# Layer 2's exponentials and logarithms from one activation table, and the layernorms' reciprocal deviation by a GpSimd power

## The chip, the cores and the metric

One core of one Trainium2 chip runs the whole program. The time is the device time of a run in microseconds (us), and a kernel's figure is the median of its runs.

## The reference, cut to what matters

Four graph layers over 4096 nodes with 256 features, each closed by a residual and a layernorm.

```
_layernorm(x) = (x - mean) / sqrt(var + 1e-5)
x = _layernorm(x + L0(x, adj))                  # attention over adj, 8 heads
x = _layernorm(x + L1(x, adj))                  # (diag + adj) @ (x @ W) + b
x = _layernorm(x + L2(x, adj))                  # two steps, below
x = _layernorm(x + L3(x, adj))                  # relu(concat(x, mean of neighbours) @ W + b)

# L2, for each of two steps:
A  = top_p(softmax(q @ k.T), 0.9)               # the largest entries of a row that sum to 0.9
Xf = R @ Xf ;  Xa = A @ Xa
Z  = Z + Xf @ U1[n].T + Xa @ U2[n].T
# after both: layernorm of X + Z with gain and bias
```

## The kernel before: the parts that matter

Layer 2 works through 32 blocks of 128 rows in each of its two steps. `scores` of block b+2, `nucleus` of block b+1 and the two products of block b are interleaved. In the profile's lines, L777 is the row sum `Zs`, L780 the logarithm that starts ScalarE's chain, L765 the chain's small functions, L866 the first use of the candidate threshold `c` on VectorE, L1058 the copy `aT` that feeds TensorE's attention products at L1061. L72 to L79 is the layernorm.

```python
def layernorm(self, pool, dst, src, gain=None, bias=None):      # L65
    ...
        nc.vector.bn_stats(stats[:, q, :], src[:, q, :])
        nc.vector.bn_aggr(mv[:, q, :], stats[:, q, :])           # L74
    std = pool.tile([P, n], F32, name="ln_std")
    nc.scalar.activation(std, mv[:, :, 1], AF.Sqrt, bias=self.eps)
    nc.vector.reciprocal(rstd, std)
    for q in range(n):
        nc.vector.tensor_scalar(dst[:, q, :], src[:, q, :], mv[:, q, 0:1], rstd[:, q:q + 1],
                                op0=ALU.subtract, op1=ALU.mult)  # L79
    ...
# layer 1, for each block
    self.adj_product(work, ps, b, lambda jc: XD[:, jc])          # TensorE, L138
    nc.gpsimd.tensor_add(xb[:, 0], xb[:, 0], row)                # L606
    nc.vector.tensor_add(xb[:, 0], xb[:, 0], ps[:, :D])          # L607
    nc.vector.tensor_add(xb[:, 0], xb[:, 0], ps[:, D:])
    self.layernorm(work, xb, xb)
    ...
# layer 2
def scores(b, above):
    product(q, e, sums=zp)                                       # logits L753, exponentials L757
    nc.vector.tensor_reduce(Z, zp, AX.X, ALU.add)                # L777, Zs
    nc.scalar.activation(t, Z, AF.Ln, scale=(1 - TOP_P) / N)     # L780
    ...                                                          # small functions, L765
    nc.scalar.activation(c1, z, AF.Exp, scale=spread[:, b:b + 1])    # L789
    ...                                                          # four passes over the row, c
def nucleus(...):
    nc.vector.scalar_tensor_tensor(c, c1, 0.3, c2, ...)          # L866
    S = evaluate("S2", c)                                        # once in step 1, twice in step 2
    ...                                                          # top 40 of a row, cut
    r = small("r")                                               # two buffers in turn
    nc.vector.tensor_reduce(r, tmp, AX.X, ALU.max)               # L928
    ...
    for j in range(M):                                           # M = 16 pieces of the mask, L947
        nc.vector.scalar_tensor_tensor(ec, ec, edge[:, j:j + 1], ec, ...)
def attention(dst, e, r):
    for g in range(NB // 4):
        ...                                                      # four transposes, L1056
        nc.scalar.copy(aT, pt)                                   # L1058
        for k in range(4):
            nc.tensor.matmul(pa[:, :D], aT[:, k * P:(k + 1) * P], X[:, jc, :], ...)   # L1061
    nc.scalar.mul(dst, pa[:, :D], r)                             # L1063, reads r
def close(step, b, two):
    terms(h[:, 0], ..., two)                                     # TensorE L1081, VectorE L1083
    if step == 1:
        self.layernorm(work, h, h, gain, lnb)
        nc.vector.tensor_add(h[:, 0], h[:, 0], xb[:, 0])
        self.layernorm(work, h, h)
        nc.scalar.dma_start(xo[...], h[:, 0])                    # L1099, issued from ScalarE's queue
    ...
```

## Time and profile before

| | us |
|---|---|
| median before, 3 runs | 5526.98 (5522.69 to 5530.19) |
| profiled span | 5533.4 |
| layer 0, to its first closing layernorm | 1737.3 |
| layer 2, step 1, first to last L866 | 1325.2 |
| layer 2, step 2, first to last L866 | 1388.0 |

Half of the kernel is layer 2, a loop over blocks. What counts there is the distance of one L866 to the next, not the busy share of an engine. A timeline line holds the start, the duration, the engine, the line, the operation, out<-in and, in brackets, the idle time ahead of it and what ended it.

### The profile page before, as it was taken

How to read it: one execution, taken by the hardware profiler on the slowest of the kernel's cores; microseconds unless marked ns; L12 is line 12 of the kernel's file. 1: busy time of each engine (PE TensorE's matmuls, PEld its weight loads, DVE VectorE, ACT ScalarE, POOL GpSimd, SP SyncE). 2: the span in 40 equal slices, each digit the busy share in tenths (PEclk: the TensorE clock that was granted, in tenths of full speed). 3: DMA queues.
4: the chain of work that ended last, by engine and by line, in shares of the span. 5: the costliest groups of instructions: out<-in, count | busy, mean ns of one | idle time of the engine just before them, and what ended most of it. 6: DMA issues, size and time to landing. Idle time of an engine off the chain costs nothing. (4 is left out here: it accounts for less than half of the span.)

```text
span 5533.4 us, 72575 instructions
## 1 busy us (share of the span) xinstructions
PE 4416.8 (80%) x25835; PEld 3505.5 (63%) x25836; DVE 3492.3 (63%) x8321; ACT 3189.8 (58%) x6086; POOL 324.7 (6%) x519
## 2 busy tenths in 40 slices
PE   6899967767774997777778887876777777777799
PEld 4699967767774873555555555634555555555677
DVE  4322258878887233866666666429888888888422
ACT  4333369879994116655556666356776767676211
POOL 3344400000000100000000000000000000000000
PEclk7899989999997998899999999988999999998999
DMA  4599953332223681111111222141111111111476
GB/s 148 187 335 343 337 194 110 131 146 89 91 94 94 223 286 43 60 64 62 62 62 63 64 70 69 55 140 38 56 56 56 56 56 56 56 56 55 148 228 204
DMA packets 333886, 655.59 MB, mean 118 GB/s; under 512 B 73537, under 2 KB 146113, under 8 KB 324289
## 3 DMA queue, kind: packets, MB, share of 16 engines
q1 hardware_dynamic: 189824, 436.29, 24.3%
q10 hardware_dynamic: 112960, 113.79, 6.3%
q0 software_dynamic: 30720, 100.69, 4.8%
q8 instruction: 208, 3.41, 0.3%
q14 instruction: 174, 1.42, 0.1%
HBM read 490.46 MB, written 160.17 MB: 118 GB/s over the span
## 5 line engine op out<-in xcount | busy, mean ns | idle before, releaser
L1061 PE MATMUL ps_a<-X,aT 128*128 128x256 f32 x4096 | 1073.9, 420 | 554.6 <-ACT aT L1058 554.5
L1061 PEld LDWEIGHTS ps_a<-X,aT 128*128 128x128 f32 x4096 | 841.4, 211 | 784.1 <-ACT aT L1058 656.9
L249 PE MATMUL acc<-gm,gt 128*128 128x198 bf16 x8192 | 747.4, 250 | 254.2 <-DVE gt L244 242.4
L242 ACT ACTIVATE sg<-lpb,lc 128x1024 bf16<-128x1024 f32 x832 | 870.9, 1134 | 119.3 <-DVE gt L244 78.9
L249 PEld LDWEIGHTS <-gt 128*128 128x128 bf16 x8192 | 693.6, 98 | 307.9 <-DVE gt L244 284.8
L1058 ACT COPY aT<-ps_tp 128x512 f32<-128x512 f32 x512 | 281.0, 581 | 640.4 <-PE ps_tp L1056 639.9
L380 PE MATMUL pz<-src,ar 128*128 128x264 f32 x4096 | 549.1, 294 | 49.2 <-ACT src L337 31.9
L244 DVE TENSOR_TENSOR gt<-sg,na 128x4096 bf16<-128x4096 bf16 x208 | 474.1, 2285 | 164.6 <-ACT sg L242 164.6
L380 PEld LDWEIGHTS pz<-src,ar 128*128 128x128 f32 x4096 | 522.7, 194 | 70.3 <-ACT src L337 42.2
L811 ACT ACTIVATE ja<-e,nc 128x2048 bf16<-128x2048 f32 x256 | 509.3, 1989 | 0.0
L138 PE MATMUL ps_r<-XD,adj_piece 128*128 128x512 f32 x2048 | 500.0, 398 | 11.2 <-DMA adj_piece<-adjs 6.6
L138 PE MATMUL ps_adj<-XD,adj_piece 128*128 128x512 f32 x2048 | 492.2, 397 | 10.2 <-DMA adj_piece<-adjs 10.2
L138 PEld LDWEIGHTS ps_r<-XD,adj_piece 128*128 128x128 f32 x2048 | 378.9, 188 | 134.5 <-DVE h L1083 28.7
L138 PEld LDWEIGHTS ps_adj<-XD,adj_piece 128*128 128x128 f32 x2048 | 383.7, 189 | 93.0 <-DVE XD L113 10.9
L841 DVE SCALAR_TENSOR_TENSOR v<-e,c 128x4096 bf16<-128x4096 f32 x96 | 429.3, 4472 | 1.1
L947 DVE SCALAR_TENSOR_TENSOR e<-e,edge 128x256 f32<-128x256 f32 x1024 | 415.0, 478 | 2.0
L753 PE MATMUL ps_logit<-kT,q 64*128 64x512 f32 x1024 | 367.7, 662 | 55.0 <-ACT e L757 53.4
L372 ACT ACTIVATE nb<-a 128x512 bf16<-128x512 f32 x256 | 158.4, 630 | 356.9 <-DMA a<-in_adjt_dram 280.9
L901 DVE MAX8 cand<-v 128x8 f32<-128x256 f32 x1024 | 355.2, 411 | 3.1
L757 ACT ACTIVATE e<-ps_logit 128x1024 f32<-128x1024 f32 x256 | 261.8, 1030 | 99.0 <-PE ps_logit L753 96.3
L1056 PE MATMUL ps_tp<-ident,e 128*128 128x128 f32 x2048 | 270.8, 274 | 40.8 <-DVE e L947 40.8
L897 DVE SCALAR_TENSOR_TENSOR v<-e,hi 128x2048 f32<-128x2048 f32 x128 | 300.8, 2350 | 2.1
(288 smaller groups left out, 4786.4 us busy)
## 6 DMA issues: line engine op xcount, KB each, us to landing
adj_piece<-adjs SPq DMA_DIRECT2D x256, 512.0 KB, 5.3
adj_piece<-adjs SPq DMA_DIRECT2D x512, 256.0 KB, 3.2
a<-in_adjt_dram SPq DMA_DIRECT2D x256, 256.0 KB, 5.8
adjs<-ar POOLq DMA_DIRECT2D x256, 256.0 KB, 5.7
na<-nad SPq DMA_DIRECT2D x64, 1024.0 KB, 6.3
nad<-nb POOLq DMA_DIRECT2D x128, 256.0 KB, 5.1
lpb<-lpd ACTq DMA_DIRECT2D x32, 512.0 KB, 5.2
gmd<-gb ACTq DMA_DIRECT2D x64, 198.0 KB, 2.2
```

The lines of the kernel that those rows point to most:

```text
L138: nc.tensor.matmul(ps, a[:, k, :], rhs(jc).rearrange("p s d -> p (s d)"), start=(jc == 0), stop=(jc == self.NB - 1))
L242: nc.scalar.activation(sg[:, k, :], lpb, AF.Sign, bias=lc[:, jc, h:h + 1])
L244: nc.vector.tensor_tensor(*flat, ALU.is_gt)
L249: nc.tensor.matmul(acc[:, q, :6 * C1], gt[:, k, q * P:(q + 1) * P], gm[:, jc, hh, :], start=(jc == 0 and q % 2 == 0), stop=(jc == NB - 1 a ...
L380: nc.tensor.matmul(pz[q][:, t, :W], ar[:, q, k, :], src[:, jc, t, s], start=(jc == 0 and s == 0), stop=(jc == NB - 1 and s == 1))
L753: nc.tensor.matmul(pl[:, s, :], q[s * A:(s + 1) * A, :], kT[s * A:(s + 1) * A, c * 512:(c + 1) * 512], start=True, stop=True)
L811: nc.scalar.activation(ja, e[:, s * HALF:(s + 1) * HALF], f, bias=nc1, accum_out=fs[:, i + s:i + s + 1])
L841: nc.vector.scalar_tensor_tensor(junk, e, c, e, op0=ALU.is_ge, op1=ALU.mult, accum_out=S)
L897: nc.vector.scalar_tensor_tensor(v, ec, hi, ec, op0=ALU.is_lt, op1=ALU.mult, accum_out=sb[:, s:s + 1])
L901: nc.vector.max(cand[:, 8 * j:8 * j + 8], v[:, k * 256:(k + 1) * 256])
L947: nc.vector.scalar_tensor_tensor(ec, ec, edge[:, j:j + 1], ec, op0=ALU.is_ge, op1=ALU.mult)
L1061: nc.tensor.matmul(pa[:, :D], aT[:, k * P:(k + 1) * P], X[:, jc, :], start=(jc == 0), stop=(jc == NB - 1))
```

## The change

ScalarE's functions come in sets, and a function outside the loaded set costs a table load (221 of them, 1.283 us each, in the profile of before). The change names the one set that serves exponential and logarithm, and takes the root, which isn't in it, away from ScalarE: GpSimd adds the epsilon and raises to the power -0.5.

```diff
-        self.eps = pool.tile([P, 1], F32, name="eps")
-        nc.vector.memset(self.eps, EPS)
+        self.power = pool.tile([P, 1], F32, name="power")
+        nc.vector.memset(self.power, -0.5)
...
-        std = pool.tile([P, n], F32, name="ln_std")
-        nc.scalar.activation(std, mv[:, :, 1], AF.Sqrt, bias=self.eps)
-        nc.vector.reciprocal(rstd, std)
+        var = pool.tile([P, n], F32, name="ln_var")
+        nc.gpsimd.tensor_scalar_add(var, mv[:, :, 1], EPS)
+        nc.gpsimd.tensor_tensor(rstd, var, self.power.to_broadcast([P, n]), ALU.pow)
...
+                nc.scalar.preload_act_table_set("natural_log_exp_and_others")
                 keys(X)
```

## The prediction

> **What bounds the kernel now.** I read the page first (busy shares), then the ScalarE groups, then the timelines of VectorE, ScalarE and TensorE over one block of each of layer 2's two steps, and last the order of instructions on each engine, before against after.
>
> ```profile
> PE 4416.8 (80%) x25835; PEld 3505.5 (63%) x25836; DVE 3492.3 (63%) x8321; ACT 3189.8 (58%) x6086; POOL 324.7 (6%) x519
> ```
>
> No engine is full, so the shares don't say what a table load is worth. The ScalarE groups give their number and price:
>
> ```profile
> L780 ACT ACT_TABLE_LOAD x64 | 82.1, 1283 | 28.2 <-DVE rest L910 27.3
> L76 ACT ACT_TABLE_LOAD x60 | 77.0, 1283 | 20.2 <-DVE ln_mv L74 19.1
> L789 ACT ACT_TABLE_LOAD x60 | 77.0, 1283 | 1.1
> ...
> L757 ACT ACT_TABLE_LOAD x20 | 25.7, 1283 | 0.4
> ...
> L765 ACT ACT_TABLE_LOAD x13 | 16.7, 1283 | 0.2
> ```
>
> With four single ones that is 221 loads of 1.283 us, 283.5 us of ScalarE. Nearly all are in layer 2 (64 blocks of 128 rows, 32 in each step). Whether they cost time depends on who waits. One block of step 1, VectorE:
>
> ```profile
> 2888.27 0.16 DVE L866 SCALAR_TENSOR_TENSOR c<-c,c 128x1 f32<-128x1 f32 x1 [0.53 <-ACT c L765]
> ...
> 2915.92 0.15 DVE L777 TENSOR_REDUCE Zs<-zp 128x1 f32<-128x4 f32 x1
> ...
> 2917.57 0.42 DVE L1070 TENSOR_TENSOR two<-XD 128x256 f32<-128x256 f32 x1
> 2921.44 0.42 DVE L1071 TENSOR_TENSOR two<-two,ps_r 128x256 f32<-128x256 f32 x1 [3.46 <-PE ps_r L138]
> ```
>
> and ScalarE after it:
>
> ```profile
> 2915.27 1.28 ACT L780 ACT_TABLE_LOAD   x1
> 2916.57 0.20 ACT L780 ACTIVATE t<-Zs 128x1 f32<-128x1 f32 x1
> ...
> 2918.63 0.39 ACT L765 ACTIVATE z<-z,qsp,t 128x1 f32<-128x1 f32 x1
> 2919.03 1.28 ACT L789 ACT_TABLE_LOAD   x1
> 2920.33 0.29 ACT L789 ACTIVATE c<-z,spread 128x1 f32<-128x1 f32 x1
> ...
> 2932.24 0.39 ACT L765 ACTIVATE c<-S,c,ri 128x1 f32<-128x1 f32 x1
> ```
>
> This is a loop over two engines. VectorE works without a gap from c (L866, 2888.27) to the row sum Zs (L777, done 2916.07): 27.8 us. Then ScalarE needs 16.6 us to make the next block's c (2932.63), and VectorE starts L866 at 2932.66. Together 44.4 us, the spacing of L866 through most of step 1. TensorE waits about 8 us in each block for ScalarE's first copy aT, which sits behind the same ScalarE chain. So the loads lie on the path.
>
> In step 2 (two evaluations per block and two layernorms) the loop is the same in kind, with four to six loads per block, and L866 comes at alternating distances of 48.6 and 43.55 us (26 blocks from 3905.70 to 5103.22, mean 46.06):
>
> ```profile
> 4322.39 0.16 DVE L866 SCALAR_TENSOR_TENSOR c<-c,c 128x1 f32<-128x1 f32 x1 [8.46 <-ACT c L765]
> ...
> 4343.86 0.14 DVE L777 TENSOR_REDUCE Zs<-zp 128x1 f32<-128x4 f32 x1
> ```
>
> **What the Trainium skill says.** (1) "ScalarE: Activation LUTs", section "What ACT_TABLE_LOAD costs": about 1283 ns for the load plus about 1380 ns of drain for every switch of set. The trace has 1283 ns exactly, but not the drain: the activation before the load at L789 ends at 2919.02, the load starts at 2919.03, and the next activation 0.02 us after it. I count 1.28 us, not 2.66. (2) Same page, "Table sets: the hidden batching unit": one set holds both exponential and logarithm, the root is in another. The trace agrees: a load stands before Ln, before Exp and before the layernorm's root, none between exponentials and the cheap functions. (3) "GPSIMD Engine Reference", section "Performance versus the Vector engine": GpSimd dispatches each instruction in software and runs a two-input add of 2048 columns in 4497 ns. Here 256 and 528 columns took 746 and 1116 ns: a line through them has 1.36 ns per column and about 0.4 us fixed, and for 128x1 only the fixed part counts. No run so far shows a power. (4) Same page, "Key points": it shares SBUF interfaces with VectorE. The trace shows signs: while GpSimd's additions ran in layer 1, VectorE's normalization (L79) took 0.61 and 1.05 us against 0.41 elsewhere.
>
> ```profile
> L345 POOL TENSOR_TENSOR v<-v,gb 128x528 f32<-128x528 f32 x32 | 35.7, 1116 | 98.8 <-ACT gb L344 98.8
> ...
> L606 POOL TENSOR_TENSOR X<-X,row 128x256 f32<-128x256 f32 x32 | 22.4, 746 | 1120.9 <-DVE row L600 1120.9
> ```
>
> **The change part by part.** In program order the changed kernel has two table loads in all, both hoisted to the start of the program; the root (144 times about 0.29 us) and VectorE's reciprocal go; two GpSimd instructions per layernorm come.
>
> *Step 1.* The steady order on ScalarE, VectorE and TensorE is that of before, instruction for instruction, less two loads per block. The second load saves its 1.28 us whole, since z, c and all that follows are one dependent chain. The first began at 2915.27, before Zs was ready (2916.07), so most of it is hidden: Ln could start at about 2916.11 instead of 2916.57, which is 0.46. Together 1.74 us per block, 44.4 to 42.65. Would another loop stop it? TensorE's: aT to the last logits' exponential is 27.25 us (2888.00 to 2915.25), Zs and its handoffs 0.25, ScalarE from Ln to aT and TensorE 14.5 without the load: 42.0, just under. 28 blocks at 1.74: -49 us.
>
> *Step 2.* Here the order does change, from a pattern of two blocks to one of one block, and the row sum L777 moves behind the first layernorm. I add up the new loop with the durations of before. VectorE from c to the second L897: 17.9 us; to L915: 5.0; from there, interleaved top-8 searches and layernorm, to the end of L777: 4.0; sum 26.9, plus a stall s1 where L79 waits for GpSimd. ScalarE from Zs: Ln and two small activations 0.9, a DMA issue, two more; then a DMA issue of xo that waits for the second layernorm's output, so that Exp starts 3.4 + s2 after Ln; from Exp to c 12.24 as before plus a 0.40 copy (L1073) that now stands there. Sum 43.0 + s1 + s2. With P the time from the statistics' end to the reciprocal deviation back on VectorE, 0.33 and 0.54 us of other VectorE work cover it: s1 = P - 0.33, s2 = P - 0.54. So the loop is 42.15 + 2P. P, an estimate: handoffs 0.2 and 0.15 (row to GpSimd in layer 1 took 0.23, GpSimd to GpSimd 0.07), the addition 0.25, the power 0.4 fixed plus 0.2 for its arithmetic: 1.2 us. The loop becomes 44.55 against 46.06: 1.5 us per block, 29 blocks, -44 us. Of about 6 us of loads per block only a quarter would come back: part was already hidden, part is given to GpSimd's round trip and to the later row sum.
>
> *Starts of the steps.* Before the first c of each step four or five loads stand in a bare ScalarE chain (2152 to 2185 and 3682 to 3715): -5 and -6.
>
> *Elsewhere.* Layer 1: in GpSimd's queue 29 of the 32 additions of L606 (0.70 us apart from 1834.9) stand before the first layernorm's power, so VectorE would wait at L79 of block 0 until about 1856.9 instead of 1841.5. The matmuls of block 3 need the PSUM buffer of block 1, which VectorE then empties at 1858 instead of 1853.8: +4.3 us, on a stretch where TensorE is the bound and can't regain it. The last layernorms of layer 1 and layer 3: +0.6 each. The layernorms between layers 0 and 1 lose 16 reciprocals of 0.15 on a nearly full VectorE: -2.
>
> Sum: -49 - 44 - 11 + 3.5 = -100.5. 5527 - 101 = 5426 us.
>
> **The rivals.** *All 284 us (5 per cent) come back.* For it: TensorE waits for ScalarE's aT 554.5 us in all. Against: the loads before Ln overlap VectorE's work, and VectorE's 27.8 us of the loop don't shrink. At most two loads per block on the path would give about 5380. *GpSimd's power is slow* (a scalar routine, P of 2 us or more): step 2's loop is then 46.2, nothing is gained there, and the time is about 5468; at P of 3 step 2 loses 2 us per block and the kernel ends near 5520. The fixed 0.4 us of an ordinary GpSimd instruction speaks for, the never-seen power neither way. *VectorE becomes the bound and hides all*: its work in step 2 is about 39.5 us per block with bubbles, in step 1 about 30, so it still idles some microseconds; this only matters if the loop falls below that.
>
> **Range and chances.** Step 1 is nearly certain (same order, measured durations), give or take 8 us. Step 2 carries the doubt: 0.1 us of P is worth 6 us of the total. P of 0.9 gives about 5408, 1.6 about 5450. Range 5400 to 5465. The 2 per cent line is at 5416, 10 us below my number: faster 0.38, same 0.60, slower 0.02.
>
> **What would show it.** Two loads in all; L866 spaced at 42.6 in step 1, with L780 starting within 0.1 us of Zs; L866 evenly spaced at 44 to 45 in step 2; VectorE idle about 0.9 us before L79, released by GpSimd; a VectorE wait of about 15 us at the first L79 of layer 1 and about 4 us of TensorE. It is wrong if step 1 moves by other than 1.7 us per block, or the power takes over 1 us.

## More of the kernel before

Every comparison with the kernel before uses runs made beside it on the same chip. Stage lengths come from the one profiled execution of each kernel, whose span lies within 7 us of the kernel's median.

## The result, and the profile after

| | median, us | range | runs |
|---|---|---|---|
| before | 5528.18 | 5522.69 to 5530.19 | 4 |
| after | 5449.53 | 5449.14 to 5451.39 | 4 |

The ratio is 0.986, 95% interval 0.9843 to 0.9877: within 2%. A ratio here is the mean time of one kernel's runs over that of the other's of the same rounds, so it isn't quite the ratio of the medians.

All 221 table loads but two are gone, and ScalarE's busy time falls by 319 us. The kernel got 79 us shorter. This table says where. It is worked out from the timelines of the two profiles: each stage ends where the next begins.

| stage | before | after | difference | predicted |
|---|---|---|---|---|
| layer 0, to its first closing layernorm | 1737.3 | 1722.8 | -14.5 | 0 |
| layer 0's closing layernorms | 32.0 | 45.0 | +13.0 | -2 |
| to layer 1's row (L600) | 65.0 | 64.2 | -0.8 | 0 |
| layer 1, to its last L607 | 230.3 | 238.8 | +8.5 | +4.3 |
| start of step 1, to its first L866 | 120.3 | 120.8 | +0.5 | -4.4 |
| step 1, first to last L866 | 1325.2 | 1284.6 | -40.6 | -49 |
| start of step 2, to its first L866 | 205.1 | 200.2 | -4.9 | -6 |
| step 2, first to last L866 | 1388.0 | 1335.2 | -52.8 | -44 |
| end of step 2 and layer 3 | 430.2 | 435.8 | +5.6 | +0.6 |
| span | 5533.4 | 5447.4 | -86.0 | -100.5 |

The first row isn't the change's work: its code is the same in both kernels, and in the fourteen profiles it took 1722.8 to 1740.5 us. The other stages sum to -71.5 us, beside 79 us between the medians, so some 7 us are assigned to no stage. The rest of this section goes through the other rows.

**GpSimd's cost.** The page of after and its groups by form (count | busy time, mean ns of one):

```profile
PE 4418.2 (81%) x25835; PEld 3512.0 (64%) x25836; DVE 3488.5 (64%) x8177; ACT 2870.9 (53%) x5723; POOL 444.1 (8%) x807
```

```profile
L77 POOL TENSOR_TENSOR ln_rstd<-ln_var,power 128x1 f32<-128x1 f32 x128 | 72.4, 566 | 10.6
...
L77 POOL TENSOR_TENSOR ln_rstd<-ln_var,power 128x2 f32<-128x2 f32 x16 | 11.9, 741 | 1.3
L76 POOL TENSOR_SCALAR ln_var<-ln_mv 128x2 f32<-128x2 f32 x16 | 6.7, 419 | 1045.0 <-DMA X<-in_x_dram 1019.2 <-DVE ln_mv L74 25.9
```

The power takes 0.57 us for one column, as estimated. The form with two columns takes 0.74 and its addition 0.42, and that is the form of layer 0's closing layernorms. One of them, before and then after:

```profile
1755.11 0.70 DVE L79 TENSOR_SCALAR X<-X,ln_mv,ln_rstd 128x256 f32<-128x256 f32 x2
```

```profile
1755.29 0.73 DVE L79 TENSOR_SCALAR X<-X,ln_mv,ln_rstd 128x256 f32<-128x256 f32 x2 [0.91 <-POOL ln_rstd L77]
```

VectorE now stands still for 0.9 us ahead of a normalization that had no wait before.

**Layer 1.** Its first layernorm and what follows it, after (GpSimd's additions, VectorE, TensorE):

```profile
1832.62 20.18 POOL L606 TENSOR_TENSOR X<-X,row 128x256 f32<-128x256 f32 x29 [65.62 <-DVE row L600]
```

```profile
1854.24 1.48 DVE L79 TENSOR_SCALAR X<-X,ln_mv,ln_rstd 128x256 f32<-128x256 f32 x1 [15.62 <-POOL ln_rstd L77]
```

```profile
1856.62 23.59 PE L138 MATMUL ps_adj<-XD,adj_piece 128*128 128x512 f32 x95 [5.14 <-issue]
```

GpSimd works through 29 additions before it comes to the first power. VectorE waits 15.6 us for it and so empties no PSUM buffer, and TensorE stops for 5.1 us. (The profile names no releaser for this stop; it is gone when the additions leave GpSimd, run adds_on_vector below.)

**Step 1.** Four L866 in a row, after:

```profile
2871.42 0.16 DVE L866 SCALAR_TENSOR_TENSOR c<-c,c 128x1 f32<-128x1 f32 x1 [0.53 <-ACT c L765]
...
2914.07 0.16 DVE L866 SCALAR_TENSOR_TENSOR c<-c,c 128x1 f32<-128x1 f32 x1 [0.53 <-ACT c L765]
...
2957.32 0.16 DVE L866 SCALAR_TENSOR_TENSOR c<-c,c 128x1 f32<-128x1 f32 x1 [0.53 <-ACT c L765]
...
3001.13 0.16 DVE L866 SCALAR_TENSOR_TENSOR c<-c,c 128x1 f32<-128x1 f32 x1 [0.53 <-ACT c L765]
```

The distances are 42.65, 43.25 and 43.81 us, and this period of three repeats through the whole step. The first is the predicted 42.65. ScalarE's part lost exactly what was predicted in all three: from the start of Zs to that of the logarithm it went from 0.65 to 0.19 us, from there to the exponential from 3.76 to 2.48. What varies is the time from L866 to Zs: 27.65, 28.26 and 28.82 us. It comes from TensorE. The first 16 attention products of the three blocks that follow:

```profile
2913.80 6.06 PE L1061 MATMUL ps_a<-X,aT 128*128 128x256 f32 x16 [6.78 <-ACT aT L1058]
...
2957.05 6.61 PE L1061 MATMUL ps_a<-X,aT 128*128 128x256 f32 x16 [6.49 <-ACT aT L1058]
...
3000.86 5.20 PE L1061 MATMUL ps_a<-X,aT 128*128 128x256 f32 x16 [5.39 <-ACT aT L1058]
```

They took 6.06, 6.61 and 5.20 us, and their blocks are the ones of 43.25, 43.81 and again 42.65; later groups of 16 take 3.72. VectorE shows how this reaches the loop, in the first and the second of these blocks:

```profile
2935.06 0.20 DVE L928 TENSOR_REDUCE r<-tmp 128x1 f32<-128x40 f32 x1 [0.16 <-ACT two L1063]
...
2978.87 0.20 DVE L928 TENSOR_REDUCE r<-tmp 128x1 f32<-128x40 f32 x1 [0.72 <-ACT two L1063]
```

L928 writes r, of which there are two buffers, and by the profile waits for ScalarE's L1063, which reads an older r once the attention products are done. After it VectorE waits 0.25 us more at L1083 for TensorE. In the blocks of 42.65 us both waits are absent. The granted clock says why the products are slow. Three stretches around the first of them (from:to, length, then the busy time of PE, weight loads, DVE, ACT, POOL; the third number from the right is PEclk):

```profile
2907.00:2911.70 4.70, 0.02 (x2) 0.00 (x0) 0.00 (x0) 4.70 (x10) 0.00 (x0) 1.00 0.00 0
2911.80:2918.40 6.60, 4.60 (x11) 3.72 (x12) 4.72 (x3) 3.18 (x12) 0.00 (x0) 0.50 0.11 42
2918.60:2922.00 3.40, 3.11 (x19) 2.58 (x18) 3.19 (x7) 1.07 (x2) 0.00 (x0) 1.00 0.00 0
```

TensorE idles from 2907.0 on. 4.7 us later the clock is halved, and it stays so for 6.8 us, well into the products that end the wait. Read in steps of 0.4 us, the halved stretches of three blocks in a row last 6.8, 10.2 and 3.4 us. The Trainium skill's page "TensorE: Matmul & The Clock Gate" (Part 1, "What's actually happening") says that the clock is halved after an idle window, and that the window is 4096 cycles at 1.2 GHz, 3413 ns, and runs free. The trace agrees: the stretches are 2, 3 and 1 times 3.41 us, and in its clock records all halved stretches of both steps begin on one grid of 3.413 us.

**Step 2.** The two layernorms of one block, after: VectorE's waits, GpSimd's pair, and ScalarE's queue:

```profile
4593.95 0.41 DVE L79 TENSOR_SCALAR h<-h,ln_mv,ln_rstd 128x256 f32<-128x256 f32 x1 [0.69 <-POOL ln_rstd L77]
...
4597.96 0.41 DVE L79 TENSOR_SCALAR h<-h,ln_mv,ln_rstd 128x256 f32<-128x256 f32 x1 [0.45 <-POOL ln_rstd L77]
```

```profile
4598.40 0.36 ACTq L1099 DMA_DIRECT2D xo<-h  x1
4598.81 0.39 ACT L765 ACTIVATE z<-z,cs,t 128x1 f32<-128x1 f32 x1 [1.48 <-DVE rest L938]
```

L74 ends at 4592.96 in this block and L79 starts at 4593.95, so P is 0.99 us (1.2 estimated). The second layernorm delays ScalarE's chain through the store's issue at L1099, as predicted. L866 comes every 44.37 us, evenly (44.55 predicted).

### The profile page after: what moved, and what is told of

Read it like the earlier page. It is cut to its first block, busy times and chain, and to the rows that moved or that the text cites. A ratio compares the mean times of both kernels' runs of the same rounds, so it can differ in the third digit from the quotient of the medians.

```text
span 5447.4 us, 72422 instructions
## 1 busy us (share of the span) xinstructions
PE 4418.2 (81%) x25835; PEld 3512.0 (64%) x25836; DVE 3488.5 (64%) x8177; ACT 2870.9 (53%) x5723; POOL 444.1 (8%) x807
## 3 DMA queue, kind: packets, MB, share of 16 engines
q8 instruction: 208, 3.41, 0.3%
## 5 line engine op out<-in xcount | busy, mean ns | idle before, releaser
L380 PE MATMUL pz<-src,ar 128*128 128x264 f32 x4096 | 549.7, 294 | 44.9 <-ACT src L337 33.0
L138 PEld LDWEIGHTS ps_adj<-XD,adj_piece 128*128 128x128 f32 x2048 | 385.3, 190 | 100.5 <-DVE XD L113 11.9
L76 POOL TENSOR_SCALAR ln_var<-ln_mv 128x1 f32<-128x1 f32 (+1 forms) x144 | 35.3, 245 | 4522.9 <-DVE ln_mv L74 1680.1
L753 PE MATMUL ps_logit<-kT,q 64*128 64x512 f32 x1024 | 350.8, 654 | 47.6 <-ACT e L757 45.9
```

The source lines that it names most:

```text
L138: nc.tensor.matmul(ps, a[:, k, :], rhs(jc).rearrange("p s d -> p (s d)"), start=(jc == 0), stop=(jc == self.NB - 1))
L380: nc.tensor.matmul(pz[q][:, t, :W], ar[:, q, k, :], src[:, jc, t, s], start=(jc == 0 and s == 0), stop=(jc == NB - 1 and s == 1))
L753: nc.tensor.matmul(pl[:, s, :], q[s * A:(s + 1) * A, :], kT[s * A:(s + 1) * A, c * 512:(c + 1) * 512], start=True, stop=True)
```

## The experiments

All twelve kernels gave correct results. The 95% interval of every ratio here is about 0.0017 to either side. So ln_exp_warm and the two mid kernels are faster by over 2%, ln_exp lies across that line, and the others are within 2% of before. Stage lengths from their profiles, in us, with the kernels before and after for comparison:

| kernel | median | ratio to before | layer 0's closing layernorms | layer 1 | step 1 | start of step 2 | step 2 | end and layer 3 |
|---|---|---|---|---|---|---|---|---|
| before | 5528.2 | 1 | 32.0 | 230.3 | 1325.2 | 205.1 | 1388.0 | 430.2 |
| after | 5449.5 | 0.986 | 45.0 | 238.8 | 1284.6 | 200.2 | 1335.2 | 435.8 |
| only_power | 5547.5 | 1.0025 | 44.9 | 239.6 | 1322.1 | 205.1 | 1376.6 | 434.8 |
| only_table | 5481.3 | 0.9901 | 31.1 | 230.3 | 1286.0 | 199.0 | 1384.1 | 432.7 |
| root_outside | 5435.3 | 0.9818 | 30.8 | 231.6 | 1287.0 | 198.6 | 1333.9 | 433.0 |
| ln_exp | 5415.9 | 0.9786 | 32.6 | 230.6 | 1285.3 | 198.7 | 1325.0 | 434.9 |
| warm | 5449.7 | 0.9854 | 44.9 | 239.2 | 1251.0 | 207.1 | 1342.3 | 444.8 |
| ln_exp_warm | 5357.5 | 0.9687 | 32.0 | 231.0 | 1252.3 | 209.2 | 1271.7 | 441.8 |
| pool_twice | 5469.0 | 0.9886 | 44.9 | 240.3 | 1285.3 | 198.7 | 1352.0 | 435.4 |
| adds_on_vector | 5442.9 | 0.9842 | 44.8 | 232.3 | 1286.7 | 198.8 | 1333.7 | 435.5 |
| zs_early | 5439.2 | 0.984 | 44.9 | 239.2 | 1269.9 | 200.5 | 1334.9 | 433.3 |
| out_on_sync | 5429.0 | 0.9818 | 44.9 | 238.8 | 1286.8 | 198.5 | 1311.0 | 435.2 |
| ln_exp_warm_mid | 5320.0 | 0.9622 | 33.3 | 230.6 | 1247.5 | 199.4 | 1263.8 | 430.3 |
| ln_exp_warm_mid_sync | 5331.7 | 0.9641 | 32.8 | 230.6 | 1245.9 | 200.8 | 1274.8 | 429.8 |

### Each part of the change alone

Power alone: the changed kernel without its preload.

```diff
-                nc.scalar.preload_act_table_set("natural_log_exp_and_others")
```

> The changed kernel without the one line that preloads the table set: the GpSimd power alone. Theory A (the two parts pay only together): layer 2's step 1 has no roots, so it keeps its two loads a block and the spacing of the kernel before, 44.37 us; step 2 loses the roots' loads but keeps those of logarithm and exponential on its path and pays two handovers to GpSimd, about 44.37 + 1.74 = 46.1 us a block, which is the 46.06 of before; the layernorms of layers 0, 1 and 3 cost their +20. So 5540 us (5530 to 5555), slower than before. Rival B (each load taken away gives its time back, whichever it is): a half of step 2's loads are gone, 29 x 0.9 = -25, so about 5520, and 5505 if the loads of roots were the dearer ones.

Measured 5547.5 us beside 5533.0 of before, ratio 1.0025 (1.0008 to 1.0041): slower by a little, as theory A said. Step 2 fell by 11 us where A had 0 and B 25, so neither is exact there. Layers 0 and 1 pay the full price.

Table alone: the kernel before with the set loaded ahead of layer 2's keys and held in that place.

```diff
+                if step == 0:
+                    tc.keep_in_program_order(nc.scalar.preload_act_table_set("natural_log_exp_and_others"))
                 keys(X)
```

> The kernel before (ScalarE's root) with the preload, held in its place ahead of the keys of layer 2's step 1: the table part alone. Theory A: step 1 runs free of loads, first to last block 1285 us in place of 1325 and the spacing in the period of three of the changed kernel; the first root of step 2 throws the set out again, so step 2 stays at 1388 us and the layernorms of layers 0 and 1 at their old cost. 5485 us (5478 to 5492). Rival B (the preload also decides what is loaded in step 2): step 2 shorter by some 25, 5460.

Measured 5481.3 us, ratio 0.9901 (0.9885 to 0.9918), with step 1 at 1286.0 as expected and step 2 hardly moved (-3.9). So by the ratios the table part alone is worth about -55 us, the power part alone +14, and both together -77. The missing 36 us are step 2: each root there throws the set out (144 of this run's 148 loads fall into step 2), so it takes both parts.

### The power only where it pays

ScalarE's root and the reciprocal come back outside layer 2's step 2. (The preload is also held in its place, as in only_table.)

```diff
+        if power:
             nc.gpsimd.tensor_scalar_add(var, mv[:, :, 1], EPS)
             nc.gpsimd.tensor_tensor(rstd, var, self.power.to_broadcast([P, n]), ALU.pow)
+        else:
+            nc.scalar.activation(var, mv[:, :, 1], AF.Sqrt, bias=self.eps)
+            nc.vector.reciprocal(rstd, var)
...
-                    self.layernorm(work, h, h, gain, lnb)
+                    self.layernorm(work, h, h, gain, lnb, power=True)
-                    self.layernorm(work, h, h)
+                    self.layernorm(work, h, h, power=True)
```

> A hybrid: ScalarE's root and VectorE's reciprocal in layers 0, 1 and 3, the GpSimd power only in the two layernorms of layer 2's step 2, the preload held in place ahead of layer 2's keys. Theory A (outside layer 2 the power only costs): layer 0's last layernorms back to 40 us (-10), layer 1 back to 230 us (-8), layer 2 as in the changed kernel, the tail -1 to -3: 5429 us (5422 to 5437). Rival B (the stages' differences of layers 0 and 1 are variation between runs): 5449, within 4 us of the changed kernel.

Measured 5435.3 us, ratio 0.9818 (0.9802 to 0.9835). The closing layernorms of layer 0 are back at 30.8 us and layer 1 at 231.6. So these two stages' +13.0 and +8.5 are the power's doing, and not variation between runs.

### No GpSimd at all

The reciprocal deviation as exp(-0.5 ln(var + eps)), two ScalarE functions of the set that is loaded anyway.

```diff
-        nc.gpsimd.tensor_scalar_add(var, mv[:, :, 1], EPS)
-        nc.gpsimd.tensor_tensor(rstd, var, self.power.to_broadcast([P, n]), ALU.pow)
+        nc.scalar.activation(var, mv[:, :, 1], AF.Ln, bias=self.eps)
+        nc.scalar.activation(rstd, var, AF.Exp, scale=-0.5)
```

> The changed kernel with the deviation's reciprocal as exp(-0.5 ln(var + eps)), two ScalarE instructions of the one set, no GpSimd and no second set anywhere. Theory A (what costs is the 0.98 us from the variance to the first use of the power, and GpSimd's queue): two small ScalarE instructions take about 0.65 us, so layers 0 and 1 come back by about 15, and step 2 gains 0.3 us at the first layernorm of a block; 5430 us (5420 to 5440). Rival B (ScalarE's queue is the dearer one: in step 2 the two extra instructions stand in its chain from Zs to the candidate c, or behind a 2.0 us pass): step 2 longer by 0.6 to 2 us a block, 5450 to 5500.

Measured 5415.9 us, ratio 0.9786 (0.977 to 0.9803), better than either theory had; whether it is 2% faster than before stays unclear. But step 2's blocks, once steady, are still 44.37 us apart, though VectorE no longer waits for the deviation. VectorE and TensorE in one of them:

```profile
4516.67 0.42 DVE L1083 TENSOR_TENSOR h<-xb,ps_r 128x256 f32<-128x256 f32 x1 [1.06 <-PE ps_r L1081]
...
4518.56 0.41 DVE L79 TENSOR_SCALAR h<-h,ln_mv,ln_rstd 128x256 f32<-128x256 f32 x1
```

```profile
4535.28 6.51 PE L1061 MATMUL ps_a<-X,aT 128*128 128x256 f32 x16 [6.13 <-ACT aT L1058]
```

A wait of 1.06 us for TensorE has taken the place of the waits for GpSimd, and the first attention products take 6.51 us, where they took 5.56 in the changed kernel's step 2 and take 3.72 at the full clock. The 10 us that step 2 did gain came in its first blocks.

### TensorE kept busy in its wait

Products that nothing uses fill TensorE's wait ahead of the attention products, which overwrite them. The edit on the changed kernel:

```diff
                 for g in range(NB // 4):
                     ...
+                    if g == 0:
+                        for _ in range(warm):                 # 24 in step 1, 28 in step 2
+                            tc.keep_in_program_order(
+                                nc.tensor.matmul(pa, XD[:, 0, 0, :P], XD[:, 1].rearrange("p s d -> p (s d)"),
+                                                 start=True, stop=True))
```

> The changed kernel with matrix products that nothing uses (24 a block in step 1, 28 in step 2, 128x512, about 0.24 us each) put into TensorE's wait of 6.5 to 8 us ahead of a block's attention products, so that it doesn't go idle; the real products overwrite theirs. Theory A (the idle halves the granted clock, the first 16 attention products then take 5.2 to 6.6 us in place of 3.72, and this wait, not the table load, now sets step 1's blocks): those products take 3.7 us in every block, step 1's spacing is an even 42.64 us in place of 42.64, 43.25, 43.81, which is -0.6 x 28 = -17 us; step 2 stays near 44.3, since there two handovers to GpSimd set it as well; in all 5432 us (5425 to 5440). Rival B (the period of three comes from the two buffers of r or from a DMA): the period of three stays and the time is 5449 or, with 300 us of more TensorE work at its limits, longer.

Measured 5449.7 us: no gain in all, which neither theory had. The stages tell it apart. Step 1 fell by 33.6 us, twice what A said, though a period of three remained (41.45, 41.64 and 42.03 us), as B said; and step 2, its start and the end together lost 23 us (+7.1, +6.9, +9.0). (The first row of the stages, layer 0, took 8 us more than in the profile of after and covers the rest.) TensorE in a block of step 1, and in the second fence in one of step 2; line numbers are shifted by five here, so that L1066 is the attention product, and L1060 are the unused ones:

```profile
2899.87 5.72 PE L1060 MATMUL ps_a<-XD 128*128 128x512 f32 x24
...
2908.48 3.72 PE L1066 MATMUL ps_a<-X,aT 128*128 128x256 f32 x16 [0.54 <-ACT aT L1063]
```

```profile
4642.96 5.41 PE L1066 MATMUL ps_a<-X,aT 128*128 128x256 f32 x16 [2.23 <-ACT aT L1063]
```

In step 1 the products that are used are back at 3.72 us. In step 2 waits of 1.2 to 2.5 us were left behind the unused ones, and 14 of them were still followed by 3.4 us at half clock, one window. The blocks there are 43.6 to 45.2 us apart, 44.38 in the mean.

The same on the kernel with exp(-0.5 ln):

> The same products in TensorE's wait, in the kernel with the deviation as exp(-0.5 ln) on ScalarE (5416 us). Theory A: there step 2's blocks are held at 44.37 us by TensorE's slow clock alone, as VectorE waits 1.06 us for TensorE ahead of L1083 and no longer for the deviation: step 2 falls to about 43.3 us a block (29 x 1.06 = -31) and step 1 to an even 42.64 (-17): 5368 us (5358 to 5385). Rival B (44.37 is set by something else that both kernels share, such as ScalarE's chain from Zs to c): step 2 stays at 44.37, and the time at 5399 or above.

Measured 5357.5 us, ratio 0.9687 (0.967 to 0.9703): 58 us less than without the products, where A said 48. Step 2 fell by 53 us, from 44.37 to 41.86 a block, where A had 43.3, and the wait for TensorE at L1083 is gone. Rival B, as worded, falls: 44.37 isn't the limit of what both kernels share. But the wait was 1.06 us and the block lost 2.51. The traces show that VectorE's order changed here too: three to six operations of the search for the largest entries and of the first layernorm, ahead of Zs in ln_exp, stand behind it now. No run takes that order in step 2 without the products, so how much of the 53 us is the clock isn't shown.

### Is step 2's length 42.15 + 2P?

One more addition of zero on GpSimd ahead of every one-column power.

```diff
+        if n == 1:
+            nc.gpsimd.tensor_scalar_add(var, var, 0.0)
         nc.gpsimd.tensor_tensor(rstd, var, self.power.to_broadcast([P, n]), ALU.pow)
```

> The changed kernel with one more GpSimd addition (of zero, 0.22 us and its handover, some 0.3 us) between the variance and the power of every layernorm of one block. Theory A (step 2's block is 42.15 + 2P, as predicted): +0.6 us a block, spacing 44.97 us, 29 x 0.6 = +17 and +3 in layer 1: 5468 us (5460 to 5475). Rival B (step 2's block is held at 44.37 = 13 clock windows by TensorE, and P lies beside it): spacing 44.37 still, 5450 to 5455.

Measured 5469.0 us, ratio 0.9886. Step 2 is 16.8 us longer, as theory A said (+17), and rival B is out. Block by block the formula doesn't hold, though: P grew from 0.99 to 1.28 us, so 2P gives +0.58, and the steady blocks grew by 0.85. They have a period of four, 45.23 us in the mean; only the shortest, 44.71, is the formula's 42.15 + 2 x 1.28. That the stage came out right is in part luck: fewer blocks, the steady ones, grew by more.

### Layer 1's queue

```diff
-                nc.gpsimd.tensor_add(xb[:, 0], xb[:, 0], row)
+                nc.vector.tensor_add(xb[:, 0], xb[:, 0], row)
```

> The changed kernel with layer 1's additions of the row on VectorE in place of GpSimd. Theory A (layer 1 is 8 us longer as GpSimd works through 29 of these additions, 20 us, ahead of its first power): the first layernorm of layer 1 waits 1 us, not 15.6, TensorE's stop of 5.1 us at the second block is gone, layer 1 takes 231 to 234 us in place of 238: 5443 us (5438 to 5447). Rival B (layer 1 loses the time in the 32 handovers of about 1 us): the first stall goes and layer 1 stays within 2 us of 238.

Measured 5442.9 us, ratio 0.9842. Layer 1 takes 232.3 us, so 6.5 of its 8.5 us were the queue of additions. TensorE's stop of 5.1 us is gone, and the first normalization waits 0.84 us, not 15.6:

```profile
1844.95 0.42 DVE L79 TENSOR_SCALAR X<-X,ln_mv,ln_rstd 128x256 f32<-128x256 f32 x1 [0.84 <-POOL ln_rstd L77]
```

### A control: VectorE's order alone

The unused products also made the scheduler move Zs ahead of three pieces of the mask on VectorE, which is worth 3 x 0.4 us by itself. This kernel takes that place of Zs without the products.

```diff
+                    if evals == 1 and j >= 9:
+                        with tc.issue_after(self.zs.ins):
+                            nc.vector.scalar_tensor_tensor(ec, ec, edge[:, j:j + 1], ec, op0=ALU.is_ge, op1=ALU.mult)
+                        continue
```

> A control for the run with products in TensorE's wait, as those also moved VectorE's order: there the sum Zs stands behind 9 pieces of the mask in step 1, in the changed kernel behind 12. Here the changed kernel gets that order alone, without the products. Theory A (TensorE's slow clock holds step 1): Zs can't come before the last logits, which stand behind TensorE's slowed attention products, so the first 16 products still take over 5 us, and the blocks shorten by 0 to 0.6 us: spacing 42.7 to 43.2, step 1 1268 to 1284 us, 5432 to 5450 in all. Rival B (the order alone made the gain of the run with products, 41.7 us a block and 1251 us): step 1 below 1258 us, 5425 or less.

Measured 5439.2 us, ratio 0.984, and step 1 1269.9 us: inside A's range and not B's. The blocks alternate between 42.11 and 43.22 us. The wait at L928 is still there (0.77 us in every other block); with the products it is gone. So the order alone gives 14.7 us of the 33.6 that step 1 gained with the products; the other 18.9 need the products.

### The store off ScalarE's queue

```diff
-                    nc.scalar.dma_start(xo[at(b)].rearrange("o p d -> (o p) d"), h[:, 0])
+                    nc.sync.dma_start(xo[at(b)].rearrange("o p d -> (o p) d"), h[:, 0])
```

> The changed kernel with the store of layer 2's result issued from SyncE's queue in place of ScalarE's, where the issue stands in the middle of the chain from Zs to c and holds it 1.5 us for the second layernorm. Theory A (this wait goes, and TensorE at its slow clock takes its place, as in the run with exp(-0.5 ln)): step 2's spacing stays at 44.37 and the store's move is worth what that run had at step 2's start, 0 to 10 us: 5440 to 5450. Rival B (step 2 is set by the handovers to GpSimd alone): -1.5 us a block, step 2 1292 us and 5407 in all.

Measured 5429.0 us, ratio 0.9818 (0.9801 to 0.9834). Both theories missed: step 2 fell by 24 us to 1311.0, where A had 0 to 10 and B 43. The wait at the store's issue was worth something, and TensorE took back a part of it (VectorE's wait at L1083 went from 0.11 to 0.72 us a block), but not at 44.37: the blocks have a period of four now, 42.70, 43.39, 43.87 and 44.12.

### What these periods have in common

The mean distance of L866 over the steady part of a step, times the blocks in its period, in windows of 3.413 us:

| kernel and step | mean, us | blocks | windows |
|---|---|---|---|
| before, step 1 | 44.40 | 1 | 13.01 |
| before, step 2 | 46.08 | 2 | 27.00 |
| after, step 1 | 43.24 | 3 | 38.00 |
| after, step 2 | 44.38 | 1 | 13.00 |
| zs_early, step 1 | 42.66 | 2 | 25.00 |
| pool_twice, step 2 | 45.23 | 4 | 53.01 |
| out_on_sync, step 2 | 43.52 | 4 | 51.00 |
| ln_exp, step 2 | 44.37 | 1 | 13.00 |
| ln_exp_warm, step 1 | 41.79 | 3 | 36.73 |
| ln_exp_warm, step 2 | 41.86 | 4 | 49.06 |

Wherever TensorE idles long enough to lose its clock in every block, the loop's period is a whole number of windows, to about one part in a thousand, in the kernel before too. With the wait filled (the last two rows) it isn't in step 1; 49.06 in step 2 is too near to 49 to tell. A plausible reading, argued and not tested by itself: a block that comes early in a window finds more of the half clock and is held, one that comes late finds less and catches up, until the loop runs in step with the window. What the experiments do show is that removing work here doesn't give its duration back; it moves the loop from one such ratio to another (13, then 38/3, then 25/2 windows a block in step 1). What sets the period of three or four that remains in the last two rows is open.

### A version that beats both

Exp(-0.5 ln), and the unused products only in blocks 3 to 29 of each step, where there is a wait to fill.

```diff
-                    attention(two[:, 1, :], e, rs.pop(b), warm=24 + 4 * step)
+                    attention(two[:, 1, :], e, rs.pop(b), warm=24 + 4 * step if 3 <= b < NB - 2 else 0)
```

> A candidate for the best: exp(-0.5 ln) on ScalarE and products in TensorE's wait, but only in blocks 3 to 29 of each step, as in the run with them in every block the starts and ends of the steps were longer (keys of step 2 +10 us, the end after step 2 +9, start of step 2 +10). Expected: those come back, 5357 - 25 = 5332 us (5322 to 5345). The rival: the starts were longer for other reasons, 5357.

Measured 5320.0 us, ratio 0.9622 (0.9606 to 0.9638): faster, the best, and 37 us below ln_exp_warm where 25 were expected. The starts and ends came back as expected (start of step 2 from 209.2 to 199.4, the end from 441.8 to 430.3). TensorE in one block of its step 2, and the clock over the wait and over the products:

```profile
4498.49 6.63 PE L1060 MATMUL ps_a<-XD 128*128 128x512 f32 x28
...
4508.53 3.72 PE L1066 MATMUL ps_a<-X,aT 128*128 128x256 f32 x16 [1.06 <-ACT aT L1063]
```

```profile
4500.00:4508.40 8.40, 7.46 (x33) 5.08 (x31) 5.94 (x16) 8.40 (x19) 0.00 (x0) 1.00 0.14 53
4508.40:4512.30 3.90, 3.77 (x18) 3.31 (x19) 2.81 (x3) 2.50 (x10) 0.00 (x0) 1.00 0.02 4
```

The same with the store on SyncE's queue:

> The same with the store of layer 2's result on SyncE's queue. If the second layernorm still holds ScalarE's chain by its 0.4 us through the store's issue: -0.4 x 27 = -11 us against the run without, 5321 us. If VectorE's own work sets step 2 by then: within 3 us of the run without.

Measured 5331.7 us, 12 us slower than without, against both expectations. TensorE's order differs in its step 2: two more of the next block's logit products stand between the attention groups, and Zs comes 26.55 us after L866 in the mean of the steady blocks, in place of 25.98. TensorE also waits at times for a piece of the adjacency, which is loaded from the queue that the store now stands in (9 waits in 20 blocks, 8.2 us, beside 3 and 1.8 us). But Zs is late in all blocks, and ln_exp, without this store, has 19 such waits, so the order is the likelier reason. Neither is tested.

## Why the prediction was right or wrong

The time, 5449.5 against 5426, was inside the range and on the right side of the 2 per cent line. Part of that is luck: the two steps of layer 2 were put at -49 and -44 and gave -40.6 and -52.8, so their errors cancel. Step by step:

- **Two loads in all, and no drain:** right.
- **Step 1, 28 x 1.74:** ScalarE's saving is exactly that in every block. The step that failed is the check on "another loop". TensorE's loop was put at 42.0 us, "just under", from the durations of before, with the first 16 products at 5.45 us as if that were their price. They are slow because of the halved clock, and what they take depends on where the block lies in the window: 5.20, 6.06 or 6.61 us after the change. And the loop that closed was another than the one checked: not over the logits, but over r. In the block of 43.25 us it is 21.26 us from the first attention product to L928, 7.27 to Zs and 14.72 to the next block's first product. So the blocks went from 44.40 to 43.24 in the mean and not to 42.65: 1.16 us a block, which is what the prediction itself had named as a sign that it is wrong ("other than 1.7"). The step still gave 40.6 of 49 us, as its first blocks and some uneven ones of before gained more. With the clock kept up and VectorE's order moved the same step takes 1251 us. A third buffer for r, which would take the wait at L928 away, was not tried.
- **Step 2, 42.15 + 2P:** the sign, P's share and the path through the store's issue were right; one more GpSimd instruction cost more a block than the formula says (0.85 us for 0.58). P was over-estimated (0.99 for 1.2), and the formula with 0.99 gives 44.13. Measured were 44.37, the 13 windows. Exp(-0.5 ln) took the waits for P off and stayed at 44.37, with a wait of 1.06 us for TensorE in their place. The gain of 52.8 for 44 is also larger because 46.06 to 44.37 is 1.69 a block and the first blocks gained more.
- **Layernorms between layers 0 and 1, -2:** wrong, +13.0. The prediction counted the reciprocals that VectorE no longer does, and for this stage not the wait for GpSimd, though it had called VectorE nearly full there. Putting the root back took 14 us off (45.0 to 30.8).
- **Layer 1, +4.3:** the mechanism was right to the microsecond (a wait of 15.6 us for about 15, TensorE's stop 5.1 for about 4), the sum too small: +8.5, of which 6.5 went when the additions left GpSimd.
- **Starts of the steps, -5 and -6** (-4.4 in the table, where layer 1's last layernorm is in the first)**:** step 2's start gave -4.9. Step 1's gave +0.5, but other kernels with the preload have 115 to 119 us there, so this one profile doesn't settle it.
- **The end, +0.6:** +5.6 in the profile. The kernels with the root in layer 3 (before, only_table, root_outside) have 430.2 to 433.0, those with the power and no unused products 433.3 to 435.8, so about 3 us may be the power's; but ln_exp, which has neither, is at 434.9, so this stays open.
- **The rivals:** "all 284 us come back" is out, and so is a power of 2 us. The third, VectorE as the bound, wasn't what happened; TensorE's clock, which did happen, was not among them.

## What to carry to other kernels

Before you sum up a loop from measured durations, ask which of them depend on the wait that you are about to shorten: here TensorE's products after an idle stretch ran at half clock, and a loop over three engines ran in whole numbers of that clock's window, so savings didn't come back one for one. Filling that wait with products that nothing uses gave 96 us (5415.9 to 5320.0), more than the 79 that the whole change gave; a part of it, not measured for step 2, is the order of VectorE that came with it. And when a small function moves to free a table, look first for a way to write it in the set that is loaded: exp(-0.5 ln) cost two ScalarE functions and no queue on another engine.

## What the Trainium skill lacked or had wrong

- "TensorE: Matmul & The Clock Gate" doesn't say that the period of a loop over several engines can come out as a whole number of its free-running windows. Here the steady periods were 13.01, 27.00, 38.00, 25.00, 51.00 and 53.01 windows.
- The same page's closing table allows gaps of TensorE up to about 3 us. Here a gap of 2.23 us was followed by 3.4 us at half clock and products of 5.41 us in place of 3.72 (run warm; in the 3.41 us before the clock fell, TensorE was busy for 1.18).
- "ScalarE: Activation LUTs", "What ACT_TABLE_LOAD costs", adds about 1380 ns of drain to a load. Here a load took 1283 ns, in most cases with about 0.02 us on either side (median of the 221 loads of before: 18 ns ahead, 12 ns behind).
- "GPSIMD Engine Reference" has figures for wide instructions. Missing are the narrow ones: an addition of 128x1 took 223 ns, a power of 128x1 566 ns, with two columns 419 and 741 ns, and the way from VectorE through both and back 0.99 us.
